# Sharing more depthwise rows with TensorE and moving small pieces of a Mamba stage between engines in a fused conv, attention, Mamba and expert kernel

## The chip, the cores and the metric

The kernel runs on one core of a Trainium2 chip. The metric is device time in microseconds (us) from the start to the end of one execution. Before the change three runs gave 4177.12, 4184.75 and 4185.21 us; the median is 4184.75 us. One more execution was taken with the hardware profiler; all lines quoted below come from it.

## What is computed

The reference takes an image x of 1 x 64 x 64 x 256 in float32 and runs two layers on it, all in float32:

```
x = x + conv_attention(groupnorm(x))      # layer 0
t = tokens(x)                             # 4096 x 256
t = t + mamba_mlp(layernorm(t))           # layer 1, two directions of a scan
t = t + experts(layernorm(t))             # layer 1, top 2 of 8 experts
```

Two parts matter here. In layer 0, q, k and v come from a 1x1, a 3x3 and a 5x5 convolution with 256 output channels each; then every channel gets its own 3x3 filter (the depthwise convolution: nine taps, each a shifted image times one number per channel, summed). In layer 1 a Mamba block runs the recurrence h[t] = exp(dt[t] A) h[t-1] + dt[t] B[t] x[t] for 512 channels x 16 states in a forward and a backward direction, and y[t] = sum over states of C[t] h[t]. Its output passes a small MLP with layer norms before and after.

## The kernel before, in words

The program is laid out by hand: every engine's queue holds its instructions in the order in which the Python code issues them, and an engine works them off in that order. There are four stages: convolutions (0 to 657 us), attention (657 to 1968 us), Mamba (1968 to about 3908 us) and experts (the rest).

**Convolution stage** (`conv_phase`). The k and v convolutions are done by Winograd's method along the width: VectorE makes transformed inputs (`inputs`, helpers `madd` L274 and `plus` L277) and transformed weights (`weights`), TensorE multiplies them (L453), VectorE combines the products into a padded image `pad` (`transform_out`). q needs only plain matmuls (L445). The work is cut into twelve units (kind, half of the image, tile of 128 channels), in the order k00, k01, k10, k11, q00, v00, q01, v01, q10, q11, v10, v11. A first half yields 24 rows of 64 pixels, a second half 40. The depthwise filter of a unit (`depthwise`, a Python generator) runs while the next unit's convolution does: at L544 ScalarE writes tap 0 into `acc`, and at L551 VectorE adds taps 1 to 8, in two pieces of half of the rows each, so sixteen instructions of 768 elements (24 rows) or 1280 (40 rows). The generator stops after each of the sixteen, and the main loop takes 18 steps of it per unit: all at once in a q unit, in four or three portions in a v or k unit.

Only the last unit, v11, gives 16 of its 40 rows to TensorE: `diagonal` makes nine 128x128 matrices with the tap's weights on the diagonal (L514, ScalarE, one buffer `diag`), and `products` (L520) sums nine matmuls of a shifted image for eight rows in a PSUM bank:

```
for tap in range(9):
    nc.tensor.matmul(ps, diag[:, tap, :], pad[shifted by tap, 8 rows], start=tap == 0, stop=tap == 8)
```

ScalarE copies the bank into `acc` (L558). When a k or q unit is finished, its rows are normalised in groups of three chunks: squares on ScalarE (L579), a matmul (L580), maximum, root and reciprocal (L587, L588 on ScalarE, L589), a matmul back (L594), a multiplication. v rows are transposed on TensorE through the single-buffered PSUM tile `tr` (L616) and copied out by ScalarE (L618). The product tiles `cv` have four PSUM banks; `feed` lets TensorE run up to three products ahead of their use.

**Mamba stage** (`mamba_phase`). There are 16 chunks i (8 blocks of 512 tokens x 2 directions, even i forward), and 32 slots per chunk, so 512 slots. In a slot: GpSimd makes `dbx` = dt B x (`inflow`, L1726, two slots ahead), ScalarE makes `da` = exp(dt A) (`decay`, L1716, one slot ahead), VectorE scans (`recur`, L1737) and multiplies by C (L1742); in five slots of each chunk (POOLED) GpSimd does this multiplication (L1747). `keep` (L1765, ScalarE) saves the last state, `sum_states` (L1774, TensorE) sums over states, and `close` (L1782, VectorE) gates the result in slots 0, 8, 16 and 24. Two sequences lie in one scan of 1024 elements; `bring` (L1757, ScalarE) adds the state kept from the chunk before to the first element of the second sequence, one slot ahead, for chunks 2 to 15: a one-element activation per slot. ScalarE also needs a table load when it changes between Exp and other functions; in slot 0 it runs two Silu on `z` (L1848).

Two generators are stepped beside the slots: `prepare` makes the inputs of the next chunk, one step per slot, and `tail` does MLP and norms of a finished block of tokens. `tail` is cut in 38 pieces of one matmul group, one activation or the like, and names with each `yield` the engine that the next piece needs. The set FULL lists the slots in which an engine takes no piece:

```
if tails and (i == 2 * NCH - 1 or at not in FULL[needs[0]]):
    needs[0] = next(tails[0], None)
```

In the last chunk (i = 15) every slot takes a piece, and what is left is drained after the last slot, before `last_output` and `last_tail`, which finish the last block alone.

Of the kernel before, what the change touches and what calls it, by code (L numbers as in the profile page):

```python
# [14 lines left out]
FP = mybir.dt.float32  # L15
# [3 lines left out]
AF = mybir.ActivationFunctionType  # L19
ALU = mybir.AluOpType  # L20
# [4 lines left out]
P = 128  # L25
# [4 lines left out]
N = 512  # L30
# [31 lines left out]
def step(gen, n=1):  # L62

    for _ in range(n):
        if gen is None or next(gen, StopIteration) is StopIteration:
            return False
    return True
# [106 lines left out]
def conv_phase(cx, xT, w1, w3, w5, temp, qd, kd, vd, uk, uv):  # L174
# [13 lines left out]
    nc, tc = cx.nc, cx.tc  # L188
# [3 lines left out]
    with ExitStack() as ctx:  # L192
# [5 lines left out]
        pcv = ctx.enter_context(tc.tile_pool(name="a_pcv", bufs=4, space=PSUM))  # L198
        pms = ctx.enter_context(tc.tile_pool(name="a_pms", bufs=1, space=PSUM))
# [51 lines left out]
        for t in range(CT):  # L251
            x = tp.tile([P, 4, 32], FP, name="px", tag="t")
# [5 lines left out]
            ps = pms.tile([P, N], FP, name="ps", tag=f"ps{t}")  # L258
# [68 lines left out]
        def inputs(kind, half):  # L327
# [86 lines left out]
        units = [("k", h, t) for h in range(2) for t in range(CT)]  # L414
        units += [("q", 0, 0), ("v", 0, 0), ("q", 0, 1), ("v", 0, 1), ("q", 1, 0), ("q", 1, 1), ("v", 1, 0), ("v", 1, 1)]
        jobs = [
            (u, i) for u in units for i in (range(4) if u[0] == "q" else PTS[u[0]])
        ]
        ready, us, ms, where = set(), {}, {}, {}
        at = {"load": 0, "job": 0, "used": 0}  # L420

# [94 lines left out]
        def products(pad, r, ps):  # L516

            for tap in range(9):
                dy, dx = divmod(tap, 3)
                nc.tensor.matmul(  # L520
                    ps.rearrange("p (h s j) -> p h s j", s=4, j=TX), diag[:, tap, :],
                    pad[:, r + dy : r + dy + 8, dx : dx + 4, :], start=tap == 0, stop=tap == 8,
                )

        def depthwise(kind, half, t, pad):

            row0, n = (LAG, H - LAG) if half else (0, LAG)
            ch = {"q": 0, "k": CT, "v": 2 * CT}[kind] + t
            dst = accp.tile([P, (H - LAG) * W], FP, name="acc", tag="acc")
            shared = 16 if (kind, half, t) == units[-1] else 0  # L530
            mine = n - shared

            def piece(b, tap):
                dy, dx = divmod(tap, 3)
                m = mine // 2
                return (
                    dst[:, m * W * b : m * W * (b + 1)].rearrange("p (h w) -> p h w", w=W),
                    pad[:, m * b + dy : m * b + dy + m, dx : dx + 4, :].rearrange("p h s j -> p h (s j)"),
                    wdw[:, 9 * ch + tap : 9 * ch + tap + 1],
                )  # L540

            for b in range(2):
                o, src, w_ap = piece(b, 0)
                nc.scalar.activation(o, src, AF.Copy, scale=w_ap)  # L544
            parts = [pcv.tile([P, N], FP, name="cv", tag="cv") for _ in range(shared // 8)]
            for i, ps in enumerate(parts):
                products(pad, mine + 8 * i, ps)
            for b in range(2):
                for tap in range(1, 9):
                    o, src, w_ap = piece(b, tap)  # L550
                    nc.vector.scalar_tensor_tensor(o, src, w_ap, o, ALU.mult, ALU.add)  # L551
                    yield
                if kind == "v":
                    m = mine * W // P // 2
                    turn(dst, t, row0 * W // P, m * b, m)
                if b == 0 and shared:
                    for i, ps in enumerate(parts):
                        nc.scalar.copy(dst[:, W * (mine + 8 * i) : W * (mine + 8 * i + 8)], ps)  # L558
                    turn(dst, t, row0 * W // P, 2 * m, shared * W // P)
            if kind != "v":  # L560
                c0 = row0 // ROWS
                rows_left.extend((dst[:, N * j : N * j + N], kind, t, c0 + j) for j in range(n // ROWS))
                if not busy:
                    busy.append(None)
                    later(norm_sums)
# [44 lines left out]
        def turn(acc, t, at0, b0, n):  # L610

            for g in range(b0, b0 + n, 4):
                m = min(4, b0 + n - g)
                ps = pms.tile([P, 4, P], FP, name="tr", tag="tr")
                for i in range(m):
                    nc.tensor.transpose(ps[:, i, :], acc[:, P * (g + i) : P * (g + i + 1)], cx.ident)  # L616
                s = tp.tile([P, 4, P], FP, name="vs", tag="t")
                nc.scalar.copy(s[:, 0:m, :], ps[:, 0:m, :])  # L618
                nc.gpsimd.dma_start(out=vd[t][:, at0 + g : at0 + g + m, :], in_=s[:, 0:m, :])
# [3 lines left out]
        def later(f, lag=1):  # L623
            events.append((clock[0] + lag, f))
# [9 lines left out]
        with tc.manual_schedule(engines=ORDERED):  # L634
# [15 lines left out]
            ps = pms.tile([P, N], FP, name="ps", tag="ps0")  # L650
# [7 lines left out]
            ps = pms.tile([P, N], FP, name="ps", tag="ps1")  # L658
# [72 lines left out]
            for n, (kind, half, t) in enumerate(units):  # L731
                pad, r0 = pads[n % 2], 9 if half else 1
# [38 lines left out]
                if not half:  # L771
                    nc.scalar.copy(edge, pad[:, LAG : LAG + 9, 1:5, :])
                before = depthwise(kind, half, t, pad)
                if n == len(units) - 2:
                    diagonal(2 * CT + units[-1][2])
# [441 lines left out]
def mamba_phase(cx, early, w_in, w_x, w_out, w1, w2, x1d, ud, bcd, dtd, x2d, u2d, usum):  # L1217
# [11 lines left out]
    nc, tc = cx.nc, cx.tc  # L1229
    with ExitStack() as ctx:  # L1230
# [314 lines left out]
        def start():  # L1545
# [57 lines left out]
            soft(3)  # L1603
            step(norm)
            inflow(0)
            decay(0)
            decay(1)
# [5 lines left out]
            for e in range(1, ET):  # L1613
                log(e)
            inflow(1)
            step(norm)
            load_bc(0, 3)
# [86 lines left out]
        SPS = ET * SQ * 2  # L1704
        firsts, first_rows, got_first, brought = {}, {}, {}, {}
        gots, bcs, dts, m_of, das, us, ys, hs = {}, {}, {}, {}, {}, {}, {}, {}
# [13 lines left out]
        def inflow(n):  # L1720

            if n >= len(slots):
                return
            i, e, k, j = slots[n]
            u = us[n] = up.tile([P, 2, N], FP, name="dbx", tag="dbx")
            nc.gpsimd.tensor_tensor(  # L1726
                u, dts[i, e, j][1], bcs[i, k][0][:, None, :].to_broadcast([P, 2, N]), ALU.mult
            )

        def recur(n):  # L1730

            i, e, k, j = slots[n]
            da, u = das[n], us.pop(n)
            h = hs[n] = hp.tile([P, 2, N], FP, name="h", tag="h")
            if n % SPS in POOLED:
                das[n] = h
            nc.vector.tensor_tensor_scan(  # L1737
                das[n].rearrange("p v n -> p (v n)"), da.rearrange("p v n -> p (v n)"),
                u.rearrange("p v n -> p (v n)"), state[i % 2][:, 4 * e + j, k : k + 1], ALU.mult, ALU.add,
            )  # L1740
            if n % SPS not in POOLED:
                nc.vector.tensor_tensor(h, da, bcs[i, k][1][:, None, :].to_broadcast([P, 2, N]), ALU.mult)  # L1742
# [3 lines left out]
            i, e, k, j = slots[n]  # L1746
            nc.gpsimd.tensor_tensor(hs[n], hs[n], bcs[i, k][1][:, None, :].to_broadcast([P, 2, N]), ALU.mult)  # L1747

        def bring(n):

            if n >= len(slots) or n in there:
                return
            there.add(n)
            i, e, k, j = slots[n]
            if i < 2:
                return
            nc.scalar.activation(  # L1757
                us[n][:, 1, 0:1], us[n][:, 1, 0:1], AF.Identity, bias=brought[i, e // 2][:, e % 2, j // 2, k : k + 1]
            )

        def keep(n):

# [17 lines left out]
        def close(i, e):  # L1780
# [9 lines left out]
        AHEAD = 5  # L1790

        LATE = {0: 0, 1: 0, 2: 0, 3: 0, 4: 0, 6: 2, 7: 6, 13: 2, 14: 2, 15: 2, 16: 2}

        FULL = {
            "PE": {0, 1, 2, 3, 4, 5, 6, 7, 9, 18, 19, 20, 21, 23, 25, 27, 29},
            "ACT": {0, 6, 7, 8, 16, 17, 18, 19, 20, 21, 22, 23, 30, 31},
            "POOL": {0, 1, 2, 4, 24, 25, 26, 27, 28, 29, 30, 31},
            "DVE": {8, 16},
            "DMA": {},
        }  # L1800
        needs = ["PE"]
        with tc.manual_schedule(engines=ORDERED):
# [5 lines left out]
            for n, (i, e, k, j) in enumerate(slots):  # L1808
# [3 lines left out]
                if at in CARRY and 1 < i + (at > 16) < 2 * NCH:  # L1812
                    carry(i + (at > 16), *CARRY[at])
                inflow(n + 2)
                if n > 0:
                    keep(n - 1)
# [32 lines left out]
                if i == 0:  # L1849
                    step(begin)  # L1850
                step(prep, LATE.get(at, 1) if i == 0 else 1)
                if at >= SPS - AHEAD and i + 2 < 2 * NCH:
# [190 lines left out]
def kernel(  # L2043
# [45 lines left out]
    nc.vector.tensor_scalar(beyond, hottest, SAFE, None, ALU.is_gt)  # L2089

    conv_phase(cx, xT, w1, w3, w5, temp, qd, kd, vd, uk, uv)
    with tc.tile_pool(name="early", bufs=1) as pool:
        early = Early(cx, pool, w_in, w_x, w_dt)
# [106 lines left out]
```

## Time and profile before

| quantity | value |
|---|---|
| median of three runs | 4184.75 us (4177.12 to 4185.21) |
| profiled execution, its own time | 4177.76 us |
| span of the profile | 4175.9 us |
| TensorE busy | 3613.0 us, 87% |
| VectorE busy | 3491.8 us, 84% |
| ScalarE busy | 2676.0 us, 64% |
| GpSimd busy | 1738.8 us, 42% |
| convolution stage, 0 to 657 us: TensorE, VectorE, ScalarE busy | 512.5, 548.2, 127.7 us |
| attention, 657 to 1968 us: TensorE, VectorE, ScalarE busy | 1286.3, 1086.9, 1046.6 us |
| Mamba chunks 2 to 15, 2202 to 3854 us: VectorE, GpSimd, TensorE, ScalarE busy | 1574.0, 1421.2, 1351.0, 1266.2 us |

In the profile PE is TensorE's matmul side, PEld its weight loads, DVE VectorE, ACT ScalarE, POOL GpSimd, SP the engine that issues most DMAs. A line of the timeline gives start, busy time, engine, source line, operation, output<-input with shape, and the number of merged instructions; in brackets stands the idle time before it and what ended that. Each float32 matmul leaves two records, so x20 are ten matmuls. A line of waits gives: waiting engine and line, the releaser, total us, number of waits, longest. A line of windows gives start:end, length, busy us of each engine (records), the granted TensorE clock, the DMA share and GB/s.

### The profile page before, as it was taken

Reading aid. Unit: us, or ns where it says so; the run is one execution under the profiler, and the core shown is the slowest. Engines: PE = TensorE matmul, PEld = TensorE weight load, DVE = VectorE, ACT = ScalarE, POOL = GpSimd, SP = SyncE. Lnnn points to the kernel's source line nnn. Section 1 sums busy time; section 2 is a strip of 40 time slices with the busy share of each in tenths; the row PEclk is TensorE's granted clock in tenths of the full one; section 3 lists DMA queues with packets and bytes.
Section 4 is the critical chain, followed back from the end, with each engine's and each line's share of the span. In section 5 each row is a group of like instructions: output and inputs, shape, how many; then the busy total and the mean of one; then the engine's idle time right before and its main releaser. Section 6 shows DMA issues by size and latency. Waiting matters only on the chain. (4 is left out here: it accounts for less than half of the span.)

```text
span 4175.9 us, 43561 instructions
## 1 busy us (share of the span) xinstructions
PE 3613.0 (87%) x15116; PEld 1180.8 (28%) x15116; DVE 3491.8 (84%) x2898; ACT 2676.0 (64%) x4187; POOL 1738.8 (42%) x1132
## 2 busy tenths in 40 slices
PE   6769789999999999998788878888888888876798
PEld 2223332222222222222222222222222222221343
DVE  8998867889889888678899999999999999998211
ACT  1111226878878878776777778778788778774222
POOL 3020000000000000001888889888888889896000
PEclk9889898999999999998888999989898999987899
DMA  6232124000000000003333344343434334341121
GB/s 207 89 110 93 55 71 134 12 26 19 19 21 19 19 21 19 11 23 108 114 107 115 113 128 134 119 134 109 135 105 119 112 129 138 116 133 54 67 69 35
DMA packets 150533, 351.20 MB, mean 84 GB/s; under 512 B 35493, under 2 KB 44453, under 8 KB 150046
## 3 DMA queue, kind: packets, MB, share of 16 engines
q1 hardware_dynamic: 139214, 313.17, 23.9%
q0 software_dynamic: 11088, 35.14, 2.4%
q8 instruction: 121, 1.98, 0.2%
q14 instruction: 110, 0.90, 0.1%
HBM read 268.69 MB, written 79.56 MB: 83 GB/s over the span
## 5 line engine op out<-in xcount | busy, mean ns | idle before, releaser
L1726 POOL TENSOR_TENSOR dbx<-dtxr,b 128x1024 f32<-128x1024 f32 x512 | 1201.6, 2358 | 231.2 <-DVE da L1737 109.0
L1010 ACT ACTIVATE e<-sc 128x1024 f32<-128x1024 f32 x1024 | 992.4, 1023 | 200.6 <-PE sc L1003 158.9
L1737 DVE TENSOR_TENSOR_SCAN da<-da,state,dbx 128x1024 f32<-128x1024 f32 x432 | 1014.1, 2347 | 40.3 <-ACT state L1765 25.6
L929 DVE TENSOR_TENSOR s<-s,e 128x1024 f32<-128x1024 f32 x768 | 880.5, 1216 | 43.9 <-ACT e L1010 43.2
L1716 ACT ACTIVATE da<-dtr,aneg 128x512 f32<-128x512 f32 x1024 | 708.1, 692 | 32.6 <-DMA dtr<-dtd 2.9
L1003 PE MATMUL sc<-q,kS 32*128 32x512 f32 x4096 | 652.7, 642 | 7.8 <-ACT e L1010 6.5
L132 POOL TENSOR_TENSOR ln_few<-ln_few,minus_half 128x4 f32<-128x4 f32 x29 | 29.6, 1020 | 1401.0 <-DMA ln_few<-ln_row 1401.0
L1742 DVE TENSOR_TENSOR h<-da,c 128x1024 f32<-128x1024 f32 x432 | 529.1, 1225 | 32.3
L936 PE MATMUL av<-e,vT 128*32 128x512 f32 x4096 | 548.4, 606 | 3.7 <-ACT o L942 3.7
L1774 PE MATMUL y<-h,sel 128*32 128x512 f32 x2048 | 384.4, 658 | 101.1 <-DVE h L1742 79.0
L453 PE MATMUL cv<-v,u 128*128 128x512 f32 x928 | 411.6, 604 | 27.5 <-DVE pad L274 13.4
L1003 PEld LDWEIGHTS sc<-q,kS 32*128 32x128 f32 x4096 | 211.3, 184 | 451.8 <-issue 229.0
L1300 PE MATMUL mm<-u,win 128*128 128x512 f32 x496 | 255.5, 662 | 76.5 <-ACT z L1407 29.1
L551 DVE SCALAR_TENSOR_TENSOR acc<-pad,wdw_s,acc 128x768 f32<-128x768 f32 (+1 forms) x192 | 235.8, 1233 | 25.6 <-ACT acc L544 19.9
L453 PEld LDWEIGHTS cv<-v,u 128*128 128x128 f32 x928 | 178.2, 194 | 259.3 <-issue 228.2
L1765 ACT COPY state<-da 128x2 f32<-128x2 f32 x431 | 68.0, 158 | 276.9 <-DVE h L1742 276.2
L1346 PE MATMUL mm<-xp,taps 128*128 128x512 f32 x480 | 215.8, 602 | 5.8 <-DVE m L1495 5.1
L929 DVE TENSOR_TENSOR s<-e 128x1024 f32<-128x1024 f32 x128 | 150.8, 1218 | 60.6 <-ACT e L1010 60.4
L936 PEld LDWEIGHTS av<-e,vT 128*32 128x32 f32 x4096 | 81.5, 108 | 395.2 <-issue 377.5
L1737 DVE TENSOR_TENSOR_SCAN h<-da,state,dbx 128x1024 f32<-128x1024 f32 x80 | 187.4, 2342 | 3.6 <-ACT dbx L1757 2.4
L1747 POOL TENSOR_TENSOR h<-h,c 128x1024 f32<-128x1024 f32 x80 | 188.5, 2356 | 2.1 <-ACT state L1765 2.1
L1774 PEld LDWEIGHTS y<-h,sel 128*32 128x32 f32 x2048 | 56.9, 113 | 399.5 <-DVE h L1742 188.3
(351 smaller groups left out, 3887.1 us busy)
## 6 DMA issues: line engine op xcount, KB each, us to landing
dtr<-dtd SPq DMA_DIRECT2D x128, 512.0 KB
dtxr<-dtd SPq DMA_DIRECT2D x128, 512.0 KB
b<-bcd SPq DMA_DIRECT2D x64, 256.0 KB
c<-bcd SPq DMA_DIRECT2D x64, 256.0 KB
dtd<-dt SPq DMA_DIRECT2D x64, 256.0 KB
dtd<-few SPq DMA_DIRECT2D x64, 256.0 KB
u<-uv SPq DMA_DIRECT2D x24, 640.0 KB
u<-ud SPq DMA_DIRECT2D x16, 512.0 KB
```

The source lines that it names most:

```text
L453: nc.tensor.matmul(rows4(ps), u[:, dy, P * ci : P * ci + P], v[:, dy : dy + HR, ci, :], start=dy + ci == 0, stop=dy == k - 1 and ci == CT - 1,
L551: nc.vector.scalar_tensor_tensor(o, src, w_ap, o, ALU.mult, ALU.add)
L929: nc.vector.tensor_tensor(z, x, y, ALU.add)
L936: nc.tensor.matmul(g.av[32 * h : 32 * h + 32, :], vT[:, kb, P * t + 32 * h : P * t + 32 * h + 32], es[h // 2][:, h % 2, :], start=kb == 0, ...
L1003: nc.tensor.matmul(ps[h // 2][:, h % 2, :], kS[r, t, P * kb : P * kb + P], q_t[r, t, :], start=True, stop=True,)
L1010: nc.scalar.activation(e, ps[i], AF.Exp)
L1300: nc.tensor.matmul(ps, win[d][:, t, P * e : P * e + P], u[:, t, ::-1] if d else u[:, t, :], start=t == 0, stop=t == CT - 1,)
L1716: nc.scalar.activation(da[:, v, :], dts[i, e, j][0][:, v, :], AF.Exp, scale=aneg[i % 2][:, a : a + 1])
L1726: nc.gpsimd.tensor_tensor(u, dts[i, e, j][1], bcs[i, k][0][:, None, :].to_broadcast([P, 2, N]), ALU.mult)
L1737: nc.vector.tensor_tensor_scan(das[n].rearrange("p v n -> p (v n)"), da.rearrange("p v n -> p (v n)"), u.rearrange("p v n -> p (v n)"), st ...
L1742: nc.vector.tensor_tensor(h, da, bcs[i, k][1][:, None, :].to_broadcast([P, 2, N]), ALU.mult)
L1774: nc.tensor.matmul(ys[i, e][32 * j : 32 * j + 32, :], cx.sel, hs[n + j // 2][:, j % 2, :], start=False, stop=k == SQ - 1,)
```

## The change

In the convolutions, four units instead of one share rows with TensorE: k11 gives 24 of its 40 rows, q00 all of its 24, q10 16 of 40, and v11 24 instead of 16. For the first three the diagonal matrices are made at the start of `depthwise`, and blocks of eight rows go through the tile `tr`: nine matmuls, then a ScalarE copy into `acc`, spread over the sixteen steps. In the built program TensorE's queue gets k11's 27 matmuls in one run in unit q00, q00's in three runs of 9 in unit v00, and q10's 18 in one run in unit q11, between products of the units named.

In Mamba, `bring` of the slots 1, 9, 17 and 24 (LONG) is done by GpSimd, right after `inflow` of the same slot, and no longer by ScalarE. FULL gains slot 24 for TensorE, 9 for ScalarE, 11 and 24 for VectorE, which shifts pieces of `tail` to other slots. With the new sets a tail that is under way runs some 15 slots later than before, and of block 6's tail the last two pieces are left for after the last slot.

```diff
+        SHARED = {("k", 1, 1): 24, ("q", 0, 0): 24, ("q", 1, 0): 16, ("v", 1, 1): 24}
...
-            shared = 16 if (kind, half, t) == units[-1] else 0
+            shared = SHARED.get((kind, half, t), 0)
             mine = n - shared
+            last = (kind, half, t) == units[-1]
+
+            def on_tensor(r):
+                ps = pms.tile([P, N], FP, name="tr", tag="tr")
+                products(pad, r, ps)
+                nc.scalar.copy(dst[:, W * r : W * (r + 8)], ps)
+
+            if shared and not last:
+                diagonal(ch)
...
-            for b in range(2):
+            for b in range(2 if mine else 0):
                 o, src, w_ap = piece(b, 0)
                 nc.scalar.activation(o, src, AF.Copy, scale=w_ap)
-            parts = [pcv.tile([P, N], FP, name="cv", tag="cv") for _ in range(shared // 8)]
+            parts = [pcv.tile([P, N], FP, name="cv", tag="cv") for _ in range(shared // 8 if last else 0)]
             for i, ps in enumerate(parts):
                 products(pad, mine + 8 * i, ps)
+            blocks = [] if last else list(range(mine, n, 8))
+            every = 16 // max(1, len(blocks))
             for b in range(2):
                 for tap in range(1, 9):
-                    o, src, w_ap = piece(b, tap)
-                    nc.vector.scalar_tensor_tensor(o, src, w_ap, o, ALU.mult, ALU.add)
+                    if blocks and (8 * b + tap - 1) % every == 0:
+                        on_tensor(blocks.pop())
+                    if mine:
+                        o, src, w_ap = piece(b, tap)
+                        nc.vector.scalar_tensor_tensor(o, src, w_ap, o, ALU.mult, ALU.add)
                     yield
...
-                if b == 0 and shared:
+                if b == 0 and last:
...
@@ def inflow(n):
+            if n % SPS in LONG:
+                bring(n, True)
...
-        def bring(n):
+        def bring(n, pool=False):
...
-            nc.scalar.activation(
-                us[n][:, 1, 0:1], us[n][:, 1, 0:1], AF.Identity, bias=brought[i, e // 2][:, e % 2, j // 2, k : k + 1]
-            )
+            x, old = us[n][:, 1, 0:1], brought[i, e // 2][:, e % 2, j // 2, k : k + 1]
+            if pool:
+                nc.gpsimd.tensor_tensor(x, x, old, ALU.add)
+            else:
+                nc.scalar.activation(x, x, AF.Identity, bias=old)
...
+        LONG = {1, 9, 17, 24}

         FULL = {
-            "PE": {0, 1, 2, 3, 4, 5, 6, 7, 9, 18, 19, 20, 21, 23, 25, 27, 29},
-            "ACT": {0, 6, 7, 8, 16, 17, 18, 19, 20, 21, 22, 23, 30, 31},
+            "PE": {0, 1, 2, 3, 4, 5, 6, 7, 9, 18, 19, 20, 21, 23, 24, 25, 27, 29},
+            "ACT": {0, 6, 7, 8, 9, 16, 17, 18, 19, 20, 21, 22, 23, 30, 31},
             "POOL": {0, 1, 2, 4, 24, 25, 26, 27, 28, 29, 30, 31},
-            "DVE": {8, 16},
+            "DVE": {8, 11, 16, 24},
```

## The prediction

> **What bounds the kernel now.** I first cut the span into stages with the view of windows (busy us of PE, PEld, DVE, ACT, POOL, then clock, DMA share, GB/s), then read each engine's timeline inside them.
>
> ```profile
> 185.00:291.00 106.00, 56.92 (x129) 23.41 (x127) 96.33 (x119) 13.58 (x21) 17.48 (x32) 0.78 0.28 93
> 291.00:413.00 122.00, 119.91 (x300) 49.90 (x300) 104.22 (x122) 21.50 (x36) 12.42 (x25) 0.98 0.28 98
> 413.00:458.00 45.00, 19.67 (x40) 7.42 (x39) 38.50 (x35) 11.98 (x20) 1.62 (x3) 0.65 0.04 16
> 458.00:612.00 154.00, 152.42 (x374) 65.03 (x374) 106.76 (x92) 39.30 (x60) 8.65 (x18) 0.98 0.23 78
> ```
>
> The reader is to see that the convolution stage has no single bound. VectorE sets 185 to 291 us (96 of 106) and 413 to 458 us; TensorE sets 291 to 413 (idle 2.1 us) and 458 to 612 us (idle 1.6 us). A mean over the stage (VectorE 548, TensorE 512 of 657 us) hides this. TensorE's timeline shows the one large hole, and VectorE's what fills it:
>
> ```profile
> 256.23 8.85 PE L453 MATMUL cv<-v,u 128*128 128x512 f32 x20 [0.83 <-ACT c L482]
> ...
> 291.15 2.09 PE L594 MATMUL ps<-rn,pick 32*128 32x512 f32 x6 [26.07 <-DVE rn L589]
> ```
> ```profile
> 259.87 25.30 DVE L551 SCALAR_TENSOR_TENSOR acc<-pad,wdw_s,acc 128x1280 f32<-128x1280 f32 x16
> ...
> 364.82 1.29 DVE L277 TENSOR_TENSOR out_t<-cv,c 128x512 f32<-128x512 f32 x2 [10.07 <-ACT c L482]
> ```
>
> TensorE waits 26 us for a reciprocal queued behind k11's depthwise. At 364.82 it is VectorE that waits 10 us: its copy `c` stands on ScalarE behind transposes that stand on TensorE behind products. The last unit is already even, 17.6 us of TensorE beside 16.7 us of VectorE:
>
> ```profile
> 630.47 17.61 PE L520 MATMUL cv<-pad,diag 128*128 128x512 f32 x36
> ```
>
> In Mamba, VectorE is busy 1574 of 1652 us between 2202 and 3854 us, so I read its waits (2000 to 3900 us) and ScalarE's timeline at one slot 2:
>
> ```profile
> DVE da L1737 <- ACT state L1765: 23.7, 15, 2.7
> DVE xc L1782 <- PE y L1774: 17.8, 10, 3.2
> DVE da L1737 <- ACT dbx L1757: 7.3, 12, 1.4
> ```
> ```profile
> 2321.68 9.29 POOL L1726 TENSOR_TENSOR dbx<-dtxr,b 128x1024 f32<-128x1024 f32 x4 [4.14 <-DMA dtxr<-dtd]
> ...
> 2324.07 0.29 ACT L1757 ACTIVATE dbx<-dbx,brought 128x1 f32<-128x1 f32 x1 [3.45 <-POOL dbx L1726]
> ...
> 2324.38 1.28 ACT L1848 ACT_TABLE_LOAD   x1
> ...
> 2330.70 2.36 DVE L1737 TENSOR_TENSOR_SCAN da<-da,state,dbx 128x1024 f32<-128x1024 f32 x1 [2.69 <-ACT state L1765]
> ```
>
> GpSimd gets its data late; ScalarE stands 3.45 us at slot 1's one-element `bring` until GpSimd is done, and two table loads, two Silu and slot 2's `decay` queue behind it; VectorE pays 2.69 us at slot 2. Sorted by slot, the scans of chunks 2 to 15 wait 23.4 us in slot 2, 5.0 in slot 1, 2.4 in slot 10, 2.3 in slot 25, and L1782 waits 9.8 us in slot 24 (odd chunks only).
>
> **What the Trainium skill says.** "FP8 and Floating Point Precision", TensorE Precision Notes: a true float32 matmul makes four passes. "TensorE: Matmul & The Clock Gate", Back-to-back issue gap: N/2.4 + 2.5 ns for a pass once warm, so my estimate is 4 x 216 = 0.86 us for N = 512. The trace agrees: ten matmuls in 8.85 us, and 18 of L520 in 17.6 us with a slow start. "PSUM — Partial Sum Buffer", Engine vs sequencer instructions: queues are strict FIFO and matmuls run in program order; the 3.45 us above is such a case. "ScalarE: Activation LUTs", What ACT_TABLE_LOAD costs: 1283 ns; the trace has 1.28 us.
>
> **The convolutions, step by step.** Eight rows cost nine matmuls, 9 x 0.866 = 7.8 us of TensorE. On VectorE an instruction takes 1.545 us at 1280 elements, 1.011 at 768 (both rows of L551), so 0.21 us + 1.04 ns an element, 0.744 at 512 (estimate from these two).
>
> k11: VectorE 16 x (1.545 - 0.744) = -12.8 us, TensorE +23.4 us and two waits of about 1 us for the single `tr` bank (a transpose group shows 0.7 us idle and then the restart). They run from 246.5 us, inside the hole: 246.5 + 25.9 = 272.4, two v products to 290.1. VectorE's reciprocal is then ready at about 280, so L594 runs at 290.1 instead of 291.15, and warm (1.1 us for 2.1; the next 20 records 17.4 us for 19.1). TensorE stands 3.8 us better at the end of these two products. ScalarE's added nine `diag` (2.7 us) and copies (0.58 us each) lie in its idle time.
>
> q00: VectorE -16 x 1.011 = -16.2 us, TensorE +23.4 us, spread among products that leave TensorE no hole until 413. I followed the queues: 310's product ends at 334 (322 before), v01's first three products at 377.8 (358.25 before). VectorE is not late anywhere in this: the last reciprocal it owes is ready at 335 for a use at 336. So the 364.82 above becomes about 384.3: **+19.5 us** for k11 and q00 together. From there VectorE runs without a gap to 439 us; its chain there is untouched, so the shift stays. Had TensorE's lead hidden it, the hole at 413 to 458 could give some back; since VectorE itself starts late at 384, I count none of it, and keep 15 us as what would come back at best.
>
> q10: VectorE -16 x (1.545 - 1.011) = -8.5 us in a stretch where it has gaps of 4 to 10 us already; TensorE +15.6 us and one bank wait, all in 458 to 612: **+16.6 us**.
>
> v11: VectorE -16 x (1.011 - 0.744) = -4.3 us, TensorE +7.8 us, and TensorE's transposes and attention's first matmul (656.77) follow in order: **+7.8 us**. Attention's loads, released by VectorE, start earlier but no wait on them is in the trace there; nothing gained. Sum: **+43.9 us**.
>
> **Mamba.** GpSimd adds 4 x 14 = 56 additions; the nearest row, L1432 (128x1), takes 0.19 us, 10.6 us in all, beside 232 us in which GpSimd waits. Queued behind each is the next `inflow`, with 2 to 5 us of lead in these slots; its cost is nothing unless GpSimd is late. ScalarE loses 56 x 0.28 us. Slot 1: the sum still waits for the late DMA, 5.0 us stay. Slot 2: in the example `decay` 1 ends at 2320.6, then 1.28 + 2.0 (Silu) + 0.14 + 1.28 + 1.42 us = 2326.8, against 2327.9 needed. Where GpSimd was on time about 0.35 us remains; over 14 chunks **-20 us**.
>
> FULL: in odd chunks the second group of MLP matmuls (3.9 us) leaves slot 22, where it delayed slot 24: **-9.8 us**. The ScalarE piece leaves slot 9 (-2.4), the two-activation piece leaves slot 24 of even chunks (-2.3). These pieces go elsewhere: the two activations (1.6 us) to slot 10 of odd chunks, where slot 13 has 1.2 us of ScalarE lead, and 2.4 us of GpSimd to slot 12, where I work out that 1.2 us of lead is left at slot 16; three VectorE pieces (0.74 each) leave these slots too, so leads shrink. I put new waits at 0.5 us x 7 = **+3.5 us**, between 0 and 3 us x 7 = 21. The tail's DMAs move with it in SP's queue: row stores now stand in slot 1 of odd chunks, ahead of slot 2's stores, with up to 3 us of waiting for ScalarE and no load due before slot 3; nothing. At the end the left-over multiplication on GpSimd (ready about 3854, 5.5 us after its DMA issue, 2.4 us long) and reduction (1.2 us) fit the 2.17 us wait before L1657; the next writer of `hn` at 3862.9 comes after its store: +0.5 us, up to 3. Sum: -20 - 9.8 - 4.7 + 3.5 + 0.5 = **-30.5 us**.
>
> **Total.** +43.9 - 30.5 = +13.4 us: 4177.76 becomes 4191.2 in the profiled execution. That execution is 7 us below the median of 4184.75, so the same change gives **about 4198 us**, 0.3% slower.
>
> **Rivals.** (a) Faster: the convolutions are bound by VectorE. For it speaks its 82 to 96% in most of the first 500 us. Then 41.8 us less VectorE work, with -30.5, give 4112 us. It decides from the point where the matmuls after 291 us (23.4 + 15.6 + 7.8 us) cost less than 31 us; against it stand 3.7 us of idle TensorE in the 276 us of two windows. 8%. (b) The waits only move in Mamba: GpSimd and ScalarE get late in odd chunks, 21 us as bounded above, so -13, and 4184.75 + 44 - 13 = 4216 us; for it speak leads of 1 to 2 us everywhere. 22%. (c) The hole at 413 to 458 gives 15 us back: 4183 us, 12%; against it speaks VectorE's unbroken run there. That the additions aren't moved at all is excluded by the program's order.
>
> **Numbers.** The forecast has 58%, 4187 to 4209 (its unknowns: new waits 0 to +10, end 0 to 3, slot 2 some 5 either way). With (b) and (c) the range is 4177 to 4222; it leaves out (a) and about as much above. About 0.2% (8 us, so 4176 and 4193) can be told from no change: slower is two thirds of the forecast and (b), 63%; within 24%; faster 13%.
>
> **What would show it.** TensorE nearly without gaps from 246 to about 433; VectorE's L277 of unit v01 near 384; attention's first matmul near 700 for 657; slot 2's scans without waits of 2 us and L1782 without any in slot 24. I am wrong if attention starts before 680, or if Mamba's chunks 2 to 15 don't take 20 us less.

## The result, and the profile after

In five runs of each, alternating, the changed kernel took 4203.3 us (4202.69 to 4204.99) and the kernel before 4183.79 us; the ratio is 1.0051, 95% interval 1.0038 to 1.0065, so 16 to 27 us slower. The profiled execution of the changed kernel took 4203.13 us, its span is 4201.2 us, 25.3 us longer than the span of before. Cut at the same events, these 25.3 us are:

| stretch | before | after | difference |
|---|---|---|---|
| start to attention's first matmul | 656.8 | 696.5 | +39.7 |
| attention, to the first scan of Mamba | 1311.6 | 1315.7 | +4.1 |
| Mamba chunks 0 and 1 | 233.6 | 236.3 | +2.7 |
| Mamba chunk 2's first scan to chunk 15's last | 1647.4 | 1627.8 | -19.6 |
| rest | 326.6 | 325.0 | -1.6 |

Attention's 4.1 us need not come from the change: in thirteen profiled executions, of the kernel before and of the twelve below, whose attention code is the same, this stretch took 1310.6 to 1315.3 us. In the changed kernel L551 is L568, L520 is L522, L594 is L611, L1737 is L1756, L1765 is L1787, L1774 is L1796, L1782 is L1804.

Windows of the kernel after, cut at the same work (columns as before):

```profile
185.00:288.50 103.50, 79.51 (x185) 33.24 (x183) 88.67 (x133) 16.58 (x38) 20.69 (x38) 0.88 0.30 97
288.50:430.00 141.50, 139.61 (x355) 58.89 (x354) 83.67 (x90) 23.86 (x41) 9.19 (x19) 1.00 0.24 84
430.00:475.00 45.00, 19.74 (x40) 7.88 (x41) 38.13 (x35) 11.99 (x20) 1.76 (x4) 0.64 0.04 15
475.00:645.00 170.00, 167.65 (x410) 71.20 (x408) 98.59 (x92) 42.27 (x72) 8.57 (x19) 0.98 0.21 71
```

Only the first stretch became shorter, by 2.5 us. The two stretches that TensorE had filled grew from 122 to 141.5 and from 154 to 170 us; TensorE is still busy in all but some 2 us of each, and VectorE's busy time in them fell by 20.5 and 8.2 us without shortening them. The third, VectorE's, kept its 45 us. TensorE's timeline of the kernel after:

```profile
246.01 7.99 PE L522 MATMUL tr<-pad,diag 128*128 128x512 f32 x18
254.68 7.99 PE L522 MATMUL tr<-pad,diag 128*128 128x512 f32 x18 [0.68 <-ACT acc L540]
263.35 7.99 PE L522 MATMUL tr<-pad,diag 128*128 128x512 f32 x18 [0.68 <-ACT acc L540]
271.18 17.33 PE L455 MATMUL cv<-v,u 128*128 128x512 f32 x40
288.44 1.13 PE L611 MATMUL ps<-rn,pick 32*128 32x512 f32 x6
...
663.37 25.61 PE L522 MATMUL cv<-pad,diag 128*128 128x512 f32 x54
...
696.46 3.78 PE L1020 MATMUL sc<-q,kS 32*128 32x512 f32 x12 [1.01 <-DMA kS<-kd]
```

and VectorE's:

```profile
259.38 12.43 DVE L568 SCALAR_TENSOR_TENSOR acc<-pad,wdw_s,acc 128x512 f32<-128x512 f32 x16
...
324.72 1.29 DVE L277 TENSOR_TENSOR out_t<-cv,c 128x512 f32<-128x512 f32 x2 [20.39 <-ACT c L484]
...
381.45 1.29 DVE L277 TENSOR_TENSOR out_t<-cv,c 128x512 f32<-128x512 f32 x2 [10.07 <-ACT c L484]
```

k11's three blocks fill the old hole, with 0.68 us at each change of the one bank; L611 follows 2.7 us earlier than before and without idle time. From there to 430 us TensorE is busy for 139.6 of 141.5 us and it is VectorE that waits: 20.39 us at 324.72 in front of a product's copy. L277 of v01 stands at 381.45 for 364.82, +16.6 us. At the end, v11's 54 records take 25.61 us beside 12.44 us of VectorE.

Mamba, VectorE's waits from 2040 to 3930 us:

```profile
DVE xc L1804 <- PE y L1796: 14.3, 8, 3.2
...
DVE h L1756 <- ACT state L1787: 8.8, 10, 1.6
...
DVE m L1552 <- PE tl L1547: 3.2, 3, 1.1
...
DVE da L1756 <- ACT state L1787: 2.2, 6, 0.8
```

The 23.7 us of slot 2 (scan `da` for the state copy) are 2.2 us now. The wait of `close` for TensorE fell only from 17.8 to 14.3, and two waits are new or larger: a scan that writes `h` (a POOLED slot) waits 8.8 us for the state copy, and L1552, a tail piece, 3.2 us for TensorE (0.5 before). Slot 2 itself, in chunk 3:

```profile
2368.28 0.19 POOL L1779 TENSOR_TENSOR dbx<-dbx,brought 128x1 f32<-128x1 f32 x1
...
2368.32 1.42 ACT L1733 ACTIVATE da<-dtr,aneg 128x512 f32<-128x512 f32 x2
...
2372.04 2.35 DVE L1756 TENSOR_TENSOR_SCAN da<-da,state,dbx 128x1024 f32<-128x1024 f32 x1
```

GpSimd is late here too, and slot 1's scan still waits 2.91 us for it. But its 0.19 us addition follows its own product at once; ScalarE no longer stands waiting for that product, has slot 2's `decay` done at 2369.7, and VectorE's scan of slot 2 at 2372.04 waits for nothing.

Sorted by slot, VectorE's idle us in chunks 2 to 15 (one execution of each kernel; slot 10, 12 and 16 with every instruction of the slot that waits), for the kernels of this text. The last column holds all idle time, with the pauses of under 0.15 us between instructions, which make up 27 to 29 us in each kernel:

| kernel | 1 | 2 | 10 | 12 | 16 | 24 | elsewhere new | all |
|---|---|---|---|---|---|---|---|---|
| before | 5.0 | 23.4 | 2.4 | 1.2 | 0 | 9.8 | | 76.9 |
| after | 2.9 | 3.6 | 4.8 | 8.2 | 8.5 | 0 | | 58.0 |
| a_mamba_only | 0.9 | 3.9 | 4.8 | 8.3 | 9.5 | 0 | | 57.4 |
| a_long_only | 5.4 | 4.0 | 3.3 | 1.2 | 0 | 6.4 | | 56.2 |
| a_full_only | 2.4 | 17.7 | 5.5 | 10.1 | 9.2 | 0 | | 77.0 |
| b_mamba_16 | 1.5 | 4.1 | 2.1 | 10.0 | 3.4 | 0 | | 51.7 |
| b_long_22 | 9.3 | 4.8 | 3.2 | 1.2 | 0 | 0 | slot 27: 11.5 | 63.7 |
| c_tail | 0.7 | 4.1 | 2.5 | 0 | 0 | 0 | slots 11, 13, 14: 17.7 | 54.3 |

### The profile page after: what moved, and what is told of

Its sections match the earlier page's. It is cut to its first block, busy times and chain, and to the rows that moved or that the text cites. A ratio compares the mean times of both kernels' runs of the same rounds, so it can differ in the third digit from the quotient of the medians.

```text
span 4201.2 us, 43908 instructions
## 1 busy us (share of the span) xinstructions
PE 3692.3 (88%) x15278; PEld 1215.0 (29%) x15278; DVE 3452.6 (82%) x2882; ACT 2671.3 (64%) x4164; POOL 1747.9 (42%) x1187
## 5 line engine op out<-in xcount | busy, mean ns | idle before, releaser
L1756 DVE TENSOR_TENSOR_SCAN da<-da,state,dbx 128x1024 f32<-128x1024 f32 x432 | 1014.2, 2348 | 19.4 <-ACT da L1733 9.1
L1796 PE MATMUL y<-h,sel 128*32 128x512 f32 x2048 | 380.6, 669 | 94.9 <-DVE h L1761 66.6
L455 PE MATMUL cv<-v,u 128*128 128x512 f32 x928 | 408.7, 600 | 26.7 <-DVE pad L274 13.4
L1317 PE MATMUL mm<-u,win 128*128 128x512 f32 x496 | 268.6, 692 | 88.8 <-ACT state L1787 29.1
L1787 ACT COPY state<-da 128x2 f32<-128x2 f32 x431 | 68.0, 158 | 263.8 <-DVE h L1761 262.7
L568 DVE SCALAR_TENSOR_TENSOR acc<-pad,wdw_s,acc 128x768 f32<-128x768 f32 (+2 forms) x176 | 194.4, 1110 | 25.0 <-ACT acc L556 19.7
L1756 DVE TENSOR_TENSOR_SCAN h<-da,state,dbx 128x1024 f32<-128x1024 f32 x80 | 187.5, 2344 | 9.9 <-ACT state L1787 8.8
L1317 PEld LDWEIGHTS mm<-u,win 128*128 128x128 f32 x496 | 105.4, 222 | 253.3 <-issue 106.0
```

Of the source, the lines that this page charges most:

```text
L455: nc.tensor.matmul(rows4(ps), u[:, dy, P * ci : P * ci + P], v[:, dy : dy + HR, ci, :], start=dy + ci == 0, stop=dy == k - 1 and ci == CT - 1,
L1317: nc.tensor.matmul(ps, win[d][:, t, P * e : P * e + P], u[:, t, ::-1] if d else u[:, t, :], start=t == 0, stop=t == CT - 1,)
L1756: nc.vector.tensor_tensor_scan(das[n].rearrange("p v n -> p (v n)"), da.rearrange("p v n -> p (v n)"), u.rearrange("p v n -> p (v n)"), st ...
L1796: nc.tensor.matmul(ys[i, e][32 * j : 32 * j + 32, :], cx.sel, hs[n + j // 2][:, j % 2, :], start=False, stop=k == SQ - 1,)
```

## The experiments

My theory after the result: in the convolutions TensorE is the bound from 246 us on, so every block of rows is paid there; in Mamba GpSimd's additions give the whole gain, and the moved tail pieces only move waits, because their matmuls stand in TensorE's queue ahead of something that VectorE needs. Each edit below is cut to the lines that set the run apart; a removed line is one of the changed kernel or of the kernel before, and what isn't named is as in the kernel before. Times are ratios to the kernel before, run alongside, times its median there (4173 to 4179 us), with the 95% interval.

### The four parts apart

**a_conv_only**: the convolutions' part alone.

> The convolutions of the changed kernel with the Mamba stage of the kernel before. Theory (TensorE bounds the convolutions after 246 us): attention's first matmul at about 696 us for 657, the whole 39 to 41 us slower than the kernel before, Mamba's chunks as before. Rival (VectorE bounds them, so that less depthwise on VectorE is a gain): 30 us or more faster. Rival (the loss is given back later, in attention or Mamba): less than 25 us slower.

Ratio 1.0106 (1.0092 to 1.0121): +44 us (38 to 51). Attention's first matmul is at 699 us, 42.5 later. The theory holds, and both rivals fall: less work on VectorE is no gain here, and the loss is not given back later.

**a_mamba_only**: the Mamba part alone.

> The Mamba stage of the changed kernel with the convolutions of the kernel before. Theory (the stage gains 20 + 9.8 + 4.7 us and loses about 18.6 us to new waits in slots 10, 12 and 16): 15 to 20 us faster, VectorE's waits in chunks 2 to 15 about 58 us for 77. Rival (the forecast's small new waits were right, and what the changed kernel lacked came from its convolutions' shift): about 30 us faster. Rival (waits only move): within 5 us of the kernel before.

Ratio 0.9969 (0.9957 to 0.9981): -13 us (-18 to -8), a little under the 15 to 20 expected. The forecast's 30 us are excluded, and so is the rival of no gain. VectorE's waits are 57.4 us, as expected. That the times give 13 where the waits differ by 19.5 may in part come from the one trace of the kernel before, because its waits in slot 2 are not the same each time: a_conv_only has the same Mamba code and 18.5 us there for 23.4, and its chunks 2 to 15 took 1639.9 us for 1647.4.

**a_long_only** and **a_full_only** split the Mamba part:

```diff
# a_long_only: FULL as before, and
+            if n % SPS in LONG:
+                bring(n, True)
# a_full_only: no LONG, and
-            "PE": {0, 1, 2, 3, 4, 5, 6, 7, 9, 18, 19, 20, 21, 23, 25, 27, 29},
-            "ACT": {0, 6, 7, 8, 16, 17, 18, 19, 20, 21, 22, 23, 30, 31},
+            "PE": {0, 1, 2, 3, 4, 5, 6, 7, 9, 18, 19, 20, 21, 23, 24, 25, 27, 29},
+            "ACT": {0, 6, 7, 8, 9, 16, 17, 18, 19, 20, 21, 22, 23, 30, 31},
...
-            "DVE": {8, 16},
+            "DVE": {8, 11, 16, 24},
```

> Only GpSimd's four additions (LONG) of the change; convolutions and FULL of the kernel before. Theory (the additions alone remove slot 2's waits, and the new waits come from the moved tail pieces): about 20 us faster; slot 2's scans wait 3 to 4 us for 23; L1782 (counted there) still waits 9.8 us in slot 24; slots 12 and 16 without new waits. Rival (the additions make GpSimd late and so cause the new waits): 0 to 8 us faster, with the waits of slots 12 and 16 already there.

> Only the moved tail pieces (FULL) of the change; convolutions and the kept state's additions of the kernel before. Theory: slot 24's 9.8 us and some 4 us of slots 10 and 25 go, 18 us of new waits in slots 10, 12 and 16 come, slot 2's 23 us stay: 0 to 6 us slower than the kernel before. Rival (the moved pieces are a gain by themselves, as forecast): 10 to 14 us faster.

The additions alone: 0.9953 (0.9942 to 0.9965), -20 us (-24 to -15). The moved pieces alone: 1.0013 (1.0005 to 1.0021), +5 us (+2 to +9). Waits of a_long_only:

```profile
DVE xc L1787 <- PE y L1779: 14.4, 10, 3.2
...
DVE da L1739 <- ACT state L1770: 4.1, 10, 1.0
```

and of a_full_only:

```profile
DVE xc L1782 <- PE y L1774: 14.4, 9, 3.2
DVE h L1737 <- ACT state L1765: 12.9, 15, 1.6
DVE da L1737 <- ACT state L1765: 12.5, 9, 2.7
```

With the additions alone the state copy's wait is down to 4.1 us and no `h` scan waits for it; slot 24 kept 6.4 us of its 9.8. With the moved pieces alone the `h` scan's 12.9 us are there, most of them in slot 12, and slot 2 still waits. In the table the pieces' row has 77.0 us in all, the kernel before 76.9: what left slot 24 stands in 12 and 16. The whole gain of the change in Mamba is LONG's.

### Why slots 12 and 16 wait

The tail's MLP has two weight matrices, w1 and w2; a "pair" or "piece" below is one group of matmuls with one of them. TensorE, ScalarE and VectorE in an even chunk of the kernel after that has the w2 piece in slot 8:

```profile
2743.85 3.78 PE L1547 MATMUL tl<-a1a,w2s 128*128 128x512 f32 x4 [3.80 <-DVE m L1552]
2747.42 3.19 PE L1547 MATMUL tl<-a1b,w2s 128*128 128x512 f32 x4
2750.55 3.63 PE L1372 MATMUL mm<-xc,wx 128*48 128x512 f32 x8
...
2754.22 0.58 ACT L1375 COPY few<-mm 48x512 f32<-48x512 f32 x1 [5.04 <-PE mm L1372]
...
2756.56 2.35 DVE L1756 TENSOR_TENSOR_SCAN h<-da,state,dbx 128x1024 f32<-128x1024 f32 x1 [1.63 <-ACT state L1787]
```

and in the next chunk, without it:

```profile
2861.62 5.33 PE L1372 MATMUL mm<-xc,wx 128*48 128x512 f32 x8 [3.81 <-ACT state L1787]
...
2866.99 0.58 ACT L1375 COPY few<-mm 48x512 f32<-48x512 f32 x1 [0.71 <-PE mm L1372]
```

The tail's eight records (four matmuls) go first, and ScalarE, whose queue holds `prepare`'s copy L1375, stands 5.04 us for 0.71; the state copy and slot 12's `decay` are behind it, and VectorE pays 1.63 us. In slot 15 of odd chunks the chain is shorter:

```profile
2650.24 3.78 PE L1536 MATMUL tl<-hn,w1s 128*128 128x512 f32 x4 [0.40 <-DVE a1a L1542]
2653.95 1.30 PE L1796 MATMUL y<-h,sel 128*32 128x512 f32 x8
...
2655.35 0.69 DVE L1804 TENSOR_TENSOR xc<-y,z 128x512 f32<-128x512 f32 x1 [1.48 <-PE y L1796]
```

The sum over states that `close` needs is queued behind the w1 pair. And the pieces cost double there. Windows of the kernel after (first two lines) give TensorE's granted clock over the w2 and w1 pieces:

```profile
2743.80:2750.60 6.80, 6.75 (x9) 2.58 (x10) 5.74 (x3) 4.70 (x10) 2.35 (x1) 0.54 0.00 0
2650.20:2654.00 3.80, 3.76 (x8) 1.23 (x12) 3.57 (x2) 3.73 (x6) 3.72 (x3) 0.50 0.01 2
```

and of the kernel before over its w2 piece in slot 22:

```profile
2640.40:2644.10 3.70, 3.70 (x9) 1.79 (x10) 3.60 (x3) 3.64 (x5) 1.83 (x1) 1.00 0.46 180
```

The same four matmuls took 3.7 us at clock 1.00 among `prepare`'s matmuls, and 6.8 us at 0.54 after 3.80 us of idle time. The Trainium skill, "TensorE: Matmul & The Clock Gate", Part 1, says that the array falls to half rate after an idle window of about 3.4 us and recovers after as long a busy one. The w2 piece's 3.80 us agree with the first; the full rate came back at 2750.05, only 6.2 us after the piece began. The w1 pair does not agree: TensorE had idled just 0.40 us before it (see the last section).

The half rate adds 3.1 us to the w2 piece and 1.8 us to the w1 pair (a w1 pair at 2586.83 us of the kernel before took 1.99 us); that is more than the 1.63 and 1.48 us that VectorE waits in these two chunks. By this estimate the same pieces in the same slots, at full rate, would not have reached VectorE there. No run separates the slot from the rate.

**b_mamba_16**: one number, against a_mamba_only.

```diff
-            "PE": {0, 1, 2, 3, 4, 5, 6, 7, 9, 18, 19, 20, 21, 23, 24, 25, 27, 29},
+            "PE": {0, 1, 2, 3, 4, 5, 6, 7, 9, 15, 18, 19, 20, 21, 23, 24, 25, 27, 29},
```

> The changed kernel's Mamba stage (convolutions of the kernel before) with one number more in FULL: slot 15 is added to the PE set, so the tail's second matmul pair w1 goes to slot 16 of odd chunks, behind the close there. Theory (slot 16's new 8.4 us come from that pair, which runs at half rate on a TensorE that has idled, ahead of the sum that the close waits for): slot 16's waits fall from 8.4 to under 1 us, slot 12's 8.2 us stay, VectorE waits about 50 us in all in chunks 2 to 15 for 57.4, the kernel about 7 us faster than with the change's own Mamba stage, 18 to 22 us faster than the kernel before. Rival (the slot waits because GpSimd or ScalarE are late there): slot 16's 8 us stay.

Ratio 0.9944 (0.993 to 0.9957): -23 us (-29 to -18) against before, some 10 us better than a_mamba_only, though the intervals touch; the waits fell by 5.7 us, from 57.4 to 51.7. `close` waits for TensorE

```profile
DVE xc L1787 <- PE y L1779: 4.9, 3, 3.2
```

for 14.2 in a_mamba_only: slot 16's 8.4 us at `close` are gone, and 2.3 us more of waiting for the addition of the kept state came in the slot's scan, so the slot keeps 3.4 us where I had expected under 1. Slot 12's wait stays (10.0), as it should if it belongs to the w2 piece. So it is shown that the w1 pair ahead of the sum made `close` wait in slot 16.

**b_long_22**: the other way round; the additions, FULL as before, and slot 22 closed for TensorE, so the second w2 group goes to slot 24, after the `close` there.

```diff
-            "PE": {0, 1, 2, 3, 4, 5, 6, 7, 9, 18, 19, 20, 21, 23, 25, 27, 29},
+            "PE": {0, 1, 2, 3, 4, 5, 6, 7, 9, 18, 19, 20, 21, 22, 23, 25, 27, 29},
```

> GpSimd's four additions with the FULL of the kernel before, to whose PE set slot 22 alone is added, so the tail's second w2 group goes to slot 24 of odd chunks, behind the close there; convolutions of the kernel before. Theory (a TensorE piece in the two slots ahead of a close, or ahead of the wx matmuls in slot 9, is what VectorE waits for): slot 24's last 6.4 us go, slots 12 and 16 get no new waits, VectorE's waits in chunks 2 to 15 fall to about 50 us, the kernel 26 to 30 us faster than before. Rival (the wait comes out in another slot, as it did with the change's FULL): 16 to 20 us faster, as with the additions alone.

Ratio 0.9987 (0.9979 to 0.9994): -5 us (-9 to -2). That is over 20 us short of what I expected. The rival named the reason, a wait that comes out in another slot, but its 16 to 20 us are missed too: 14 us of a_long_only's gain went, of which the waits account for 7.5 (63.7 for 56.2). Its waits:

```profile
DVE ln_xc L116 <- PE tl L113: 11.5, 6, 2.8
DVE da L1739 <- POOL dbx L1762: 9.1, 6, 2.3
```

and TensorE, in slots 24 to 26 of chunk 5:

```profile
2646.69 3.52 PE L1530 MATMUL tl<-a1a,w2s 128*128 128x512 f32 x4 [3.80 <-DVE m L1535]
2650.04 1.88 PE L1530 MATMUL tl<-a1b,w2s 128*128 128x512 f32 x4
2651.76 3.60 PE L1300 MATMUL mm<-u,win 128*128 128x512 f32 x8
...
2657.14 1.99 PE L113 MATMUL tl<-m,mean_mat 128*128 128x512 f32 x4
```

Slot 24's 6.4 us are gone as expected, but all that follows in the tail is two slots later: the norm's mean stands behind `prepare`'s matmuls, and `ln_xc`, which FULL lets VectorE take one slot after it, waits 1.3 to 2.8 us in six chunks. Why slot 1 waits 9.3 us for GpSimd (5.4 in a_long_only) I did not follow.

### The convolutions by unit

**b_k11**, **b_k11_16**, **c_q00**:

```diff
# b_k11
+        SHARED = {("k", 1, 1): 24, ("v", 1, 1): 16}
# b_k11_16
+        SHARED = {("k", 1, 1): 16, ("v", 1, 1): 16}
# c_q00
+        SHARED = {("q", 0, 0): 24, ("v", 1, 1): 16}
```

> Only k11's 24 rows on TensorE, everything else as before. Theory (its 27 matmuls fit TensorE's hole of 26 us, after which TensorE is the later one): L594 at about 288 us for 291, warm, so 2 to 4 us faster than before. Rival (VectorE decides and its 12.8 us are all gained): 10 to 13 us faster.

> Only k11, but 16 of its 40 rows on TensorE in place of 24 (VectorE's 16 instructions then have 768 elements for 1280: 16 x 0.534 = 8.5 us less; TensorE 15.6 us in its hole of 26). Theory: VectorE still ends last, its reciprocal and with it L594 at about 282.6 us for 291.2, the kernel 8 to 10 us faster than before and 5 to 7 us faster than with 24 rows. Rival (TensorE is late in any case, or the gain is given back before 440 us): 0 to 4 us faster.

> Only q00's 24 rows on TensorE (VectorE 16.2 us less), everything else as before. Theory (from 291 us on TensorE has no hole, so 27 matmuls are paid there in full): L277 of unit v01 at about 387 us for 364.8, the kernel 20 to 24 us slower than before. Rival (VectorE decides): 10 us or more faster. Rival (TensorE's lead hides them until its next hole at 413 us): within 8 us of the kernel before.

k11 alone: 0.9987 (0.998 to 0.9994), -5 us (-8 to -3), a little more than expected; VectorE's L277 of v01 stands at 359.89, 4.9 us earlier, and that is all of the 12.8 us that VectorE was spared. With 16 rows: 0.9977 (0.9966 to 0.9988), -10 us (-14 to -5). The time fits the expectation, its profile doesn't. TensorE and VectorE of b_k11_16:

```profile
285.70 1.13 PE L611 MATMUL ps<-rn,pick 32*128 32x512 f32 x6 [1.41 <-DVE rn L606]
...
321.05 3.21 PE L447 MATMUL cv<-xpad,wq 128*128 128x512 f32 x4 [2.39 <-DVE pad L274]
...
359.90 1.29 DVE L277 TENSOR_TENSOR out_t<-cv,c 128x512 f32<-128x512 f32 x2 [10.07 <-ACT c L484]
```

L611 is 5.5 us earlier, but TensorE then waits for VectorE's `pad` at 321.05, and L277 of v01 is at 359.90, where it also is with 24 rows. The intervals of the two overlap; which number of rows is better stays open.

q00 alone: 1.0047 (1.0032 to 1.0062), +20 us (13 to 26), with L277 of v01 at

```profile
386.21 1.29 DVE L277 TENSOR_TENSOR out_t<-cv,c 128x512 f32<-128x512 f32 x2 [10.32 <-ACT c L484]
```

for 364.82: +21.4 us for 25 us of added matmuls, although VectorE had 16.2 us less to do. Little of it is hidden before the hole at 413 us, and little is given back there: attention's first matmul is 19 us later.

### Versions made from this

**c_tail**: other FULL sets for the changed kernel's Mamba part, none of whose tail matmuls stands in slots 8, 15, 22 or 24.

```diff
-            "PE": {0, 1, 2, 3, 4, 5, 6, 7, 9, 18, 19, 20, 21, 23, 24, 25, 27, 29},
-            "ACT": {0, 6, 7, 8, 9, 16, 17, 18, 19, 20, 21, 22, 23, 30, 31},
+            "PE": {0, 1, 2, 3, 4, 5, 6, 7, 8, 9, 15, 18, 19, 20, 21, 23, 24, 25, 27, 29},
+            "ACT": {0, 6, 7, 8, 16, 17, 18, 19, 20, 21, 22, 23, 30, 31},
...
-            "DVE": {8, 11, 16, 24},
+            "DVE": {8, 16, 24},
```

> The changed kernel's Mamba stage with other FULL sets (slots 8 and 15 added for PE, 9 taken out for ACT, 11 for DVE), so that no matmul of the tail stands in slots 8 or 15; convolutions of the kernel before. Theory (slots 12 and 16 wait for these matmuls alone, and the two w2 groups, in slots 28 and 30 of odd chunks now, have two slots each before their result is used): VectorE's waits in chunks 2 to 15 fall from 57 us to 40 to 45, the kernel 27 to 33 us faster than before. Rival (a wait that leaves one slot comes out in another, here slots 26 to 31 of odd chunks): 15 to 22 us faster.

Ratio 0.9958 (0.9945 to 0.9972): -18 us (-23 to -12), the rival's number, though not in the slots that it named. Slots 12, 16 and 24 wait 0 us now. Other pieces moved as well here, but together with the timeline above, in which nothing of the tail but the w2 piece stands ahead of L1372, this settles slot 12's cause. Slots 11, 13 and 14, however, wait 17.7 us. ScalarE and VectorE in chunk 5:

```profile
2606.22 0.29 ACT L1764 ACTIVATE dbx<-dbx,brought 128x1 f32<-128x1 f32 x1 [2.09 <-POOL dbx L1726]
...
2606.55 2.36 DVE L1739 TENSOR_TENSOR_SCAN da<-da,state,dbx 128x1024 f32<-128x1024 f32 x1 [0.99 <-ACT dbx L1764]
```

In odd chunks the two activations came to slot 9 and GpSimd's 2.35 us addition of the tail to slot 11, one slot earlier each; GpSimd is late for slot 14, ScalarE's addition of the kept state waits 2.09 us for it, VectorE 0.99 us. The waits of slots 11 and 13 end with ScalarE's addition too; I did not follow them further.

**c_tail_k11** and **c_tail_four** put convolutions to it:

```diff
# c_tail_k11
+        SHARED = {("k", 1, 1): 24, ("v", 1, 1): 16}
# c_tail_four
+        SHARED = {("k", 1, 0): 16, ("k", 1, 1): 16, ("v", 0, 1): 8, ("v", 1, 1): 16}
...
+                elif b == 0 and shared and kind == "v":
+                    turn(dst, t, row0 * W // P, 2 * m, shared * W // P)
```

> The Mamba stage with these FULL sets, and k11's 24 rows on TensorE; q00, q10 and v11 as before. Theory (the parts add): 5 us faster than with the FULL sets alone, 32 to 38 us faster than before.

> The same Mamba stage, and only such depthwise rows on TensorE as lie in stretches that VectorE sets: 16 rows each of k10 and k11 and 8 of v01 (with the turn of these rows added), v11 16 as before. Theory (VectorE is the later one from 185 to 291 us and from 413 to 458 us): k10 gives 4 to 8 us, v01 4 us, on top of k11's 5: the kernel 40 to 48 us faster than before. Rival (k10's matmuls stand in TensorE's queue ahead of products that VectorE waits for): 30 to 37 us faster.

c_tail_k11: 0.9941 (0.9928 to 0.9955), -25 us (-30 to -19), 7 us better than c_tail for the 5 expected; it misses its 32 to 38 by what c_tail missed. c_tail_four: 0.9917 (0.9903 to 0.9931), 4142.47 us, **-35 us** (-41 to -29), the fastest of all. This too is short of the 40 to 48 expected and inside the rival's 30 to 37, by what c_tail missed: against c_tail it is 17 us better, for the 13 to 17 expected of its convolutions. VectorE of c_tail_four:

```profile
354.23 1.29 DVE L277 TENSOR_TENSOR out_t<-cv,c 128x512 f32<-128x512 f32 x2 [10.32 <-ACT c L484]
...
431.17 12.44 DVE L568 SCALAR_TENSOR_TENSOR acc<-pad,wdw_s,acc 128x512 f32<-128x512 f32 x16 [5.89 <-ACT acc L556]
...
616.96 16.70 DVE L568 SCALAR_TENSOR_TENSOR acc<-pad,wdw_s,acc 128x768 f32<-128x768 f32 x16 [6.42 <-ACT acc L556]
```

L277 of v01 is 10.6 us earlier than before, v11's depthwise (632.00 before) 15.0 us: k10 and k11 give 10.6, and the rest comes after that point, where only v01's rows are new; no run has v01 alone. The same way of sharing that costs 44 us in the changed kernel's units gains 15 in these. I did not run it with b_mamba_16's sets, which came out some 5 us better than c_tail's, though with overlapping intervals.

## Why the prediction came out as it did

It said 4198 us, 0.3% slower; measured are 0.51% (0.38 to 0.65) and 4203.3 us. The sign and the mechanism of the larger half were right, one term of the smaller half was several times too small. That the total comes so near is in part luck: between the two profiled executions the span grew by 25.3 us (19.5 between the medians) where the sum said 13.4; the convolutions cost 4 us less than said, and the median before from which 4198 was reckoned lies 7 us above the profiled execution.

**The convolutions, +43.9: right.** +39.7 us in the profile after, +44 us (38 to 51) by a_conv_only. k11 and q00: 16.6 us (19.5 said), as k11 alone gained 4.9 us, not 3.8, and q00 alone cost 21.4, not the 23.4 of its matmuls. q10: attention's preparation up to v11 moved from +16.6 to +32.9 us, so +16.3 (16.6 said). v11: 6.8 (7.8 said). Small slips of the working changed nothing: the estimate of 0.744 us for VectorE at 512 elements measured 0.777 (12.43 us for 16), "the next 20 records" after L594 are 20 matmuls in 40 records, k11's 23.4 us and two waits make 25.4, not 25.9, and two thirds of 58% with (b)'s 22% make 61%, not 63%. Rival (a), VectorE as bound, would have made q00 alone a gain; it cost 20 us. Rival (c), 15 us back in the hole at 413 us, gave nothing: the windows show that stretch at 45 us in both kernels.

**Slot 2, -20: right.** -19.8 us in these two traces, and -20 us (-24 to -15) by a_long_only, which holds the additions alone. The price of the additions, 0.19 us, and that GpSimd hides them, held. The 23.4 us of the one trace that I reckoned from lie at the upper end: five further executions with before's additions on ScalarE (one of them a_full_only) gave 17.7 to 21.7 us.

**FULL, -9.8 - 4.7 + 3.5 = -11: wrong.** The -9.8 of slot 24 came in full, of the -4.7 of slots 10 and 25 only 2.3 (`da` and `h` scans 4.7 to 2.4). But "I put new waits at 0.5 us x 7 = +3.5" measured 18.6: slot 12 +7.0, slot 16 +8.4, L1552 in slot 10 +3.2. That term lay within the 0 to 21 that I gave it, and I chose its low end for a wrong reason: I looked for leads of ScalarE and GpSimd only. Of the matmul groups I said what they leave, slot 22, and never where they arrive: the second w2 group in slot 8 of even chunks, a w1 pair in slot 15 of odd ones. Both arrive ahead of something that VectorE needs, and where TensorE ran at half rate (granted clock 0.54 and 0.50). By a_full_only the whole of FULL is +5 us (+2 to +9). The signs that I had named could not show this miss: slot 24 has no wait, as said, and chunks 2 to 15 took 19.6 us less, all but the 20 that I had set as limit, where the sum called for 31.

**Rival (b)**, "the waits only move in Mamba", had the size of the Mamba half right: -13 said, -13 (-18 to -8) by a_mamba_only. The engine it named, GpSimd and ScalarE late in odd chunks, is not the one: it is TensorE. (In c_tail's sets GpSimd is late in slot 14.) With the conv half of 44 it gives 4216, which is outside the result; a_conv_only and a_mamba_only add to +31 us where the whole has +21 (16 to 27). Their intervals, 6 and 5 us either way, just leave room for that, and no profile shows a place where the two parts help each other; it stays open.

**The end, +0.5:** -1.6 us, within what executions of the same code differ by.

## What to carry to other kernels

Moving work to an engine is paid by the stretch: rows given to TensorE cost 44 us in a set of units most of which stand where it had almost no idle time, and another set gained 15 us where VectorE ended last, in a stage whose mean busy shares (548 and 512 us of 657) told neither. When a piece of side work is moved, follow it to where it arrives, on its own engine's queue: name what stands behind it there and who waits for that, and take its duration at the rate which that engine has at that place. A list of allowed slots for one engine moves the pieces of all the others too, so a stall that leaves one slot has to be looked for in all of them; the additions here, a tiny operation done on the engine that is waited for anyway, cost no new wait in slots 12 and 16.

## What the runs showed of the hardware

TensorE ran at half rate without a long idle time before it. In chunk 5 of the kernel after, the granted clock was 1.00 up to 2637.4 us and fell to 0.50 there, 0.8 us into a pause of 1.75 us; the eight records after the pause took 1.94 us for 1.06 elsewhere. The clock stayed at 0.50 until 2654.5 us, although TensorE was busy for 15.8 of these 17.1 us. The page named above gives about 3.4 us for both ways; here the fall came after less idle time, and the recovery after far more work.

Counted over chunks 2 to 15 in both traces, after 1.6 to 1.8 us without a matmul 16 of 35 next matmul records took over 0.9 us, after 3.5 to 5 us 36 of 41. The length of the gap alone does not sort the short ones: where the last matmul before it was one of L1392's (L1375 before), which the timeline gives as 16*128, so 16 rows of the array, 9 of 12 were slow, after others 7 of 23. Whether it is these small matmuls that keep the rate down, no run here tests.
